# A decoder layer on one core: rounding attention's output on VectorE, with the order around it changed

## Chip, core and metric

The kernel runs on one core of a Trainium2 chip. The metric is device time in microseconds (us) for one execution. Its engines are TensorE (PE in the profile; PEld are its weight loads), VectorE (DVE), ScalarE (ACT), GpSimd (POOL) and SyncE (SP), which issues all transfers here. Each engine takes its instructions in program order and waits on semaphores for the others.

## What is computed

One pre-norm decoder layer on x of 8 batches x 112 tokens x 512, with a context of 8 x 375 x 512. Only the second sublayer matters here: two attentions of 16 heads of 128 (8 groups of two heads) over quantised projections, "own" over the 112 tokens and "context" over the 375, whose outputs are divided by a smoothing vector, rounded to 8-bit floats and projected together.

```python
def _div_clamp_fp8(x, scale):
    y = jnp.clip(x.astype(jnp.float32) / scale, -448.0, 448.0)
    y = y.astype(jnp.bfloat16).astype(jnp.float32)
    return y.astype(jnp.float8_e4m3fn).astype(jnp.float32)
...
core = _gqa(q, k, v).reshape(b, s, nh * d)       # own
xout = _gqa(qx, kx, vx).reshape(b, s, nh * d)    # context
cat = jnp.concatenate([core, xout], axis=-1)
catq = _div_clamp_fp8(cat, proj_smooth)
return jnp.einsum('bsi,oi->bso', catq, wproj) * (proj_in_scale * proj_w_scale)
...
x = x + _L0_attn_ref(_layernorm(x), ...)
x = x + _L0_xattn_ref(_layernorm(x), ctx_2048, ...)
x = x + _L0_ffn_ref(_layernorm(x), ...)          # silu(gate) * up, rms norm, down; ternary weights
```

## The kernel before

The program runs in stages. First attention and the quantising of its normed output (to about 180 us), then 32 *own* units (to about 460 us), 32 *context* units (to about 1,080 us), a short drain of the last ones, and the feed-forward part with its final scaling and stores.

**Units.** Unit i is head pair-of-groups s = i // 8 and batch b = i % 8. Eight units of one s are called a block here. The 896 tokens make 7 tiles of 128 (NT = 7), so a tile overlaps two batches: projection, normalising and rounding go by tiles (b = 7 has none, and the first unit of a block has no finished tile to round), scores and softmax by batches. While unit g projects, older units are advanced: `advance(stage, g)` runs that stage for each live unit that is far enough (the number beside the stage's name in `stages`). The calls stand in `Own.project` and `Context.project`; since the order is written out by hand, their order is the order of every engine's instructions.

**One own unit g before, in order.** Project q (8 matmuls of 512 columns); *rounded* of unit g-4; *normed* of g-1 (ACT: six scalings, one copy of v); statistics of q (DVE, L173 and L174); *score* of g-2 (4 matmuls, then the maximum, L847); *out* of g-5 (8 matmuls, then the addition to x, L713); *turn_p* of g-3 (transposes of the probabilities, ACT copy L866); project k and v; statistics of k, then powers on POOL (L184, L187, L133, L189); *weigh* of g-2 (four exponentials on ACT, L855, reciprocal L736 on DVE, product L738 on POOL); *attend* of g-3 (2 matmuls, `smoothed` on DVE, L747); *turn* of g-1 (transposes of q and k, L725 and L828; ACT makes qT, L730; DVE makes kT, L833); then `own_background`, which splits weight chunks of 128 x 512 into a high and a low part, and `form_parts`, which prepares the context in DRAM (ACT L1058, POOL L1059, DVE L1065). A chunk (s, what, k) has what = 0 (q), 1 (k and v) or 2 (output). Chunks with what = 2 cost ACT L300 and POOL L301; the others ACT L309 and DVE L310; those of what = 1 of the context (s > 3) ACT L293, POOL L294 and, a unit later in `split_end`, DVE L284 and ACT L285.

**Rounding before** (`rounded`, with `round_begin` and `round_a`): ACT takes the absolute value of y, scaled, into `big` (L203); DVE clips y (L207) and clips `big` (L208); POOL adds (L210) and subtracts (L758), which gives `cq`, the left operand of *out*'s matmuls.

**Buffers and queues.** PSUM has four banks with the tag ps and four with the tag pa. A ps tile takes the bank whose last use was released first, so the transposes of k (L828) wait for L713 of the same unit. Weight chunks are loaded by SP in the order of `queue`, one per finished split, five ahead.

**Drain and feed-forward.** After the last unit three passes run the remaining stages; `between` puts `ffn_input(0)` (norm, transposes, split of the feed-forward's input for the first four tiles) and four `hidden_part` calls among them, and `ffn_input(1)` follows. In the last `down`, the root-mean-square factor `rstd` comes from POOL, and DVE then does two instructions per tile (L1414 scales the partial sum and adds x, L1415 adds the last product), seven tiles, each stored at once.

Of the kernel before, what the change touches and what calls it, by code (L numbers as in the profile page):

```python
# [39 lines left out]
def decoder_layer(  # L40
# [210 lines left out]
    for s in range(8):  # L251
        if s == 4:

            for b in range(B - 1):
                queue += made.get(b, [])
                queue += [(4, 2, b)] if b < 2 else [(4, 2, 2), (4, 2, 3)] if b == 2 else [(5, 1, b - 3)]
            queue += [(5, 0, k) for k in range(KC)]
            continue
        queue += [(s, 2, k) for k in range(KC)]
        if s == 3:  # L260
            queue += [(4, 0, 0), (4, 1, 0), (4, 0, 1), (4, 0, 2), (4, 0, 3), (4, 1, 1), (4, 1, 2), (4, 1, 3)]
        elif s < 3:
            queue += [(s + 1, 1, 0), (s + 1, 1, 1), (s + 1, 0, 0), (s + 1, 0, 1)]
            queue += [(s + 1, 0, 2), (s + 1, 0, 3), (s + 1, 1, 2), (s + 1, 1, 3)]
        elif s < 7:
            queue += [(s + 1, what, k) for what in (1, 0) for k in range(KC)]

# [105 lines left out]
    with ExitStack() as st:  # L373
# [199 lines left out]
            nc.vector.tensor_mul(lnb[:, cut], rins[:, cut], vec[:, V_LNB : V_LNB + 4])  # L573
        rsm = const.tile([P, 32], F32, tag="rsm", name="rsm")
        nc.vector.reciprocal(rsm, vec[:, V_SM : V_SM + 32])
        nc.vector.tensor_scalar_mul(rsm[:, 0:16], rsm[:, 0:16], vec[:, V_SC + 2 : V_SC + 3])
        psc = const.tile([P, 1], F32, tag="psc", name="psc")
        nc.vector.tensor_mul(psc, vec[:, V_SC + 5 : V_SC + 6], vec[:, V_SC + 4 : V_SC + 5])
# [161 lines left out]
    def smoothed(u, po):  # L740

        po3 = po[:, :SH].rearrange("p (h s) -> p h s", s=S)
        r = rsm[:, 4 * u.s : 4 * u.s + 4].rearrange("p (h o) -> p h o", o=1)
        for t, rows, cut in batch_pieces(u.b):
            if (u.s, t) not in ys_:
                ys_[u.s, t] = w2.tile([P, 4, P], BF, tag="f8y", name=uid("y"), bufs=3)
            nc.vector.tensor_tensor(  # L747
                ys_[u.s, t][:, :, rows], po3[:, :, cut],
                r.to_broadcast([P, 4, cut.stop - cut.start]), ALU.mult,
            )  # L750

    def rounded(u):
        if u.b == 0:
            return
        y = ys_.pop((u.s, u.b - 1)).rearrange("p h s -> p (h s)")
        t, big = round_a(*round_begin(y, w2, 2), w2, 2)
        u.cq = w2.tile([P, 4 * P], F32R, tag="cq", name=uid("cq"))
        nc.gpsimd.tensor_tensor(u.cq, t, big, ALU.subtract)  # L758

    class Unit:  # L760

# [5 lines left out]
    class Own(Unit):  # L767
# [5 lines left out]
        def project(self, g):  # L773
            tile_ = self.b < NT
            tokens = slice(self.b * P, (self.b + 1) * P)
            if tile_:
                project_q(self, lambda k: xq[0][:, k, tokens])
                if self.i == 0:
                    quantise_turn(KC)
            advance("rounded", g)  # L780
            advance("normed", g)
            if tile_:
                heads = self.heads = Heads("own", P, 6)
                heads.stats(*[self.pq[:, j * P : (j + 1) * P] for j in range(4)])
            advance("score", g)
            advance("out", g)
            advance("turn_p", g)
            self.pkv = pa()
            for m in (0, 1) if tile_ else (1,):
                rows, n = (tokens, P) if m == 0 else (slice(self.b * S, (self.b + 1) * S), S)  # L790
                cut = slice(m * 256, (m + 1) * 256)
                for k in range(KC):
                    both(
                        self.pkv[:n, cut], xq[1 + m][:, k, rows], split[self.s, 1, k], cut,
                        k == 0, k == KC - 1,
                    )
            if self.b == NT:
                drop(self.s, 1)
            if tile_:
                heads.stats(*[self.pkv[:, j * P : (j + 1) * P] for j in range(2)])  # L800
                heads.powers([(4, epsc[:, 0:1]), (2, epsc[:, 1:2])])
            advance("weigh", g)
            advance("attend", g)
            advance("turn", g)
            if self.i < 4 * B - 1:
                own_background(self.s, self.b)
            form_parts(self.i)
# [275 lines left out]
    def own_background(s, b):  # L1083

        split_end()
        if s > 0 and b < 4:
            split_chunk(s, 2, b)
        elif s == 0 and b == 3:
            split_chunk(s, 2, 0)
            split_chunk(s, 2, 1)  # L1090
        elif s == 0 and b in (4, 5):
            split_chunk(s, 2, b - 2)
        if s < 3 and b in (4, 5):
            split_chunk(s + 1, 1, b - 4)
        if s == 3:
            for what, k in {4: ((0, 0), (1, 0)), 5: ((0, 1), (0, 2)), 6: ((0, 3), (1, 1)), 7: ((1, 2), (1, 3))}.get(b, ()):
                split_chunk(4, what, k)
                if b == B - 1:
                    split_end()
            return  # L1100
        if b >= 5:
            split_chunk(s + 1, 0, b - 5)
        if b == 7:
            split_chunk(s + 1, 0, 3)
            split_chunk(s + 1, 1, 2)
            split_chunk(s + 1, 1, 3)


    NU = FF // 256
# [103 lines left out]
                nc.gpsimd.tensor_scalar_mul(d[k], ts[k // 2][:, k % 2, :], 2.0)  # L1213
        wfs[what, i] = d

    def ffn_input(half):
        cols = CUTS[half]
        n, hs = cols.stop - cols.start, []
        for i in range(n // P):
            t = cols.start // P + i  # L1220
            h = f0.tile([P, H], F32, tag="sg", name=uid("h"), bufs=4)
            norm_apply(h, xs[t], *stats3[t])
            hs.append(h)
        for k in range(KC):
            tp = ps()
            for i, h in enumerate(hs):
                nc.tensor.transpose(tp[:, i * P : (i + 1) * P], h[:, k * P : (k + 1) * P], ident)
            hi, lo = [ring.tile("AB", "h3T", n) for _ in range(2)]
            nc.scalar.copy(hi, tp[:, :n])
            nc.vector.tensor_tensor(lo, tp[:, :n], hi.bitcast(F32), ALU.subtract)  # L1230
            hT[half, k] = hi, lo
# [124 lines left out]
    def hidden(u, pool):  # L1356
# [3 lines left out]

    hidden(0, f0)

    between = {
        (1, "score"): lambda: ffn_input(0),
        (2, "out"): lambda: hidden_part(0, 0, 0),
        (2, "turn_p"): lambda: hidden_part(0, 1, 0),
        (2, "rounded"): lambda: hidden_part(1, 0, 0),
        (3, "out"): lambda: hidden_part(1, 1, 0),
    }
    for n in range(1, 4):  # L1370
        live = [v for v in live if v.at < len(v.stages)]
        for stage in ("normed", "weigh", "out", "turn_p", "attend", "turn", "rounded", "score"):
            advance(stage, len(units) - 1 + n)
            if (n, stage) in between:
                between[n, stage]()

    attention.close()
    f1 = ctx.enter_context(tc.tile_pool(name="f1", bufs=1))
    tpool.append(ctx.enter_context(tc.tile_pool(name="tern2", bufs=1)))
    ffn_input(1)  # L1380
    expand_w("down", 0)
    ys = [f1.tile([P, H], F32, tag=f"y{t}", name=f"y{t}") for t in range(NT)]
    def down(c, hid, last):
        wd, pos = wfs.pop(("down", c)), []
        for t in range(NT):
            po = ps()
            for k in range(4):
                for part_ in range(2):
                    nc.tensor.matmul(  # L1389
                        po,  # L1390
                        lhsT=hid[part_][:, k, t * P : (t + 1) * P],
                        rhs=wd[k],
                        start=(k == 0 and part_ == 0),
                        stop=(k == 3 and part_ == 1),
                    )
            if c == 0:
                nc.vector.tensor_copy(ys[t], po)
            elif not last:
                nc.vector.tensor_tensor(ys[t], ys[t], po, ALU.add)
            else:  # L1400
                pos.append(po)
            if last and t == 1:
                pr = ps()
                for i in range(NT):
                    nc.tensor.matmul(
                        pr[:, i : i + 1], lhsT=sq[:, i * P : (i + 1) * P], rhs=ones1, start=True, stop=True
                    )
                rstd = sm("rms", NT)
                nc.vector.tensor_scalar(rstd, pr[:, 0:NT], 1.0 / FF, RMS_EPS, ALU.mult, ALU.add)
                power(rstd)  # L1410
            while last and t > 0 and pos:
                i = t + 1 - len(pos)
                r = rstd[:, i : i + 1]
                nc.vector.scalar_tensor_tensor(ys[i], ys[i], r, xs[i], ALU.mult, ALU.add)  # L1414
                nc.vector.scalar_tensor_tensor(ys[i], pos.pop(0), r, ys[i], ALU.mult, ALU.add)  # L1415
                nc.sync.dma_start(out=out[i * P : (i + 1) * P, :], in_=ys[i])

# [120 lines left out]
```

## Time and profile before

| what | before |
|---|---|
| median of 3 runs | 1285.07 us (1284.45 to 1289.41) |
| profiled execution | 1283.86 us, span 1282.1 us |
| granted TensorE clock, mean | 0.975 |
| L828 in own unit 9 to L828 in own unit 17 | 267.11 to 334.55 us |
| L828 in own unit 17 to that in own unit 25 | 334.55 to 401.89 us |
| L207 (clip of y), 128x512, between 215 and 460 us | x25, mean 1076 ns, 26.9 us |
| L210 and L758 (POOL's two steps of rounding), 128x512 | x56 each, mean 1240 and 1164 ns |

A group line of the profile reads: line, engine, operation, output tile <- input tiles, shapes, count | busy us, mean ns | idle time of the engine just before these instructions and what ended it. A row of the timeline reads: start in us, duration in us, engine, line, operation, tiles and shapes, count [idle before it <- what ended the idle]. A duration includes what an instruction waits after it has begun. A row of the waits reads: who waited <- for whom: us in total, times, longest.

### The profile page before, as it was taken

To read this page: it belongs to the slowest core of one execution; us is meant where nothing else is said; L and a number is where in the kernel's file an instruction comes from. 1 tells how busy PE (TensorE), PEld (TensorE's weight loads), DVE (VectorE), ACT (ScalarE), POOL (GpSimd) and SP (SyncE) were. 2 spreads that over 40 slices of the span, in tenths; PEclk is the share of its full clock that TensorE was granted. 3 is DMA by queue.
4 is the path that set the end of the run, shared out by engine and by line. 5 is a ranking of instruction groups with operands and counts; after the bars stand their busy time and mean duration, and the time that the engine had idled before them with its cause. 6 is when DMAs were issued, how large, how long until landed. Compare 5 with 4: busy or idle time off the path is not lost. (4 is left out here: it accounts for less than half of the span.)

```text
span 1282.1 us, 19634 instructions
## 1 busy us (share of the span) xinstructions
PE 1200.6 (94%) x6326; PEld 962.4 (75%) x6326; DVE 931.8 (73%) x2366; ACT 815.8 (64%) x2008; POOL 846.1 (66%) x938
## 2 busy tenths in 40 slices
PE   8997976889999889999999999999999998899998
PEld 5673765777888767888788778788777786687876
DVE  6647986887888866677776776677777775579864
ACT  2334676878687757667667767777667665456432
POOL 6657866687877756765767656667566655477762
PEclk9988886999999999999999999999999999999999
DMA  5001120213332354455554455554544440133201
GB/s 172 1 1 42 34 91 17 83 50 106 131 127 93 122 209 152 147 201 194 182 174 151 151 171 174 162 170 161 174 150 148 167 157 5 34 107 104 73 29 58
DMA packets 55511, 149.85 MB, mean 117 GB/s; under 512 B 6400, under 2 KB 15744, under 8 KB 55408
## 3 DMA queue, kind: packets, MB, share of 16 engines
q1 hardware_dynamic: 55408, 148.59, 35.3%
q8 instruction: 50, 0.82, 0.3%
q14 instruction: 53, 0.43, 0.1%
HBM read 120.18 MB, written 26.56 MB: 114 GB/s over the span
## 5 line engine op out<-in xcount | busy, mean ns | idle before, releaser
L912 PE MATMUL pa<-wx,ct 128*125 128x512 f32 x1152 | 289.4, 400 | 2.4 <-ACT wx L293 1.5
L912 PEld LDWEIGHTS pa<-wx,ct 128*125 128x125 f32 x1152 | 208.9, 186 | 51.2 <-ACT wx L293 1.9
L210 POOL TENSOR_TENSOR f8t<-y,big 128x512 f32<-128x512 bf16 (+1 forms) x88 | 107.4, 1224 | 140.2 <-DVE big L208 139.8
L738 POOL TENSOR_TENSOR p<-p,ri 112x448 f32<-112x448 f32 (+1 forms) x64 | 118.1, 1846 | 35.6 <-DVE ri L736 35.4
L923 DVE TENSOR_TENSOR kv<-kv,pa 125x512 f32<-125x512 f32 x96 | 65.9, 687 | 98.7 <-PE pa L912 52.2
L691 PE MATMUL pa<-hi,xq 128*128 128x512 f32 (+2 forms) x352 | 112.9, 345 | 11.0 <-DVE xq L368 9.2
L997 ACT ACTIVATE p<-ps,cmx 112x375 f32<-112x375 f32 x128 | 71.8, 574 | 75.5 <-DVE cmx L996 75.5
L1256 PE MATMUL pa<-h3T,wf 128*128 128x512 f32 (+1 forms) x512 | 110.0, 371 | 2.7 <-DVE sg L1266 2.7
L691 PE MATMUL pa<-lo,xq 128*128 128x512 f32 (+2 forms) x352 | 107.5, 331 | 0.9 <-DVE lo L310 0.9
L1256 PEld LDWEIGHTS pa<-h3T,wf 128*128 128x128 f32 x512 | 92.9, 188 | 14.9 <-DVE sg L1266 3.6
L174 DVE BATCH_NORM_AGGREGATE mv<-bst 128x2 f32<-128x6 f32 (+1 forms) x472 | 86.0, 182 | 16.3
L691 PE MATMUL ps<-hi,cq 128*128 128x512 f32 x224 | 90.8, 405 | 2.8 <-POOL cq L758 1.1
L730 ACT ACTIVATE qT<-ps,hln 128x448 f32<-128x448 f32 (+6 forms) x112 | 57.4, 567 | 56.1 <-PE ps L725 55.8
L691 PE MATMUL ps<-lo,cq 128*128 128x512 f32 x224 | 88.4, 395 | 0.0
L173 DVE BATCH_NORM_STATS2 bst<-pa 128x6 f32<-128x128 f32 x280 | 76.2, 272 | 16.2 <-PE pa L691 16.2
L988 PE MATMUL ps<-kT,qT 128*112 128x375 f32 x256 | 86.0, 478 | 0.5 <-ACT kT L974 0.5
L1158 POOL TENSOR_TENSOR th<-th,tw 128x512 bf16<-128x512 bf16 x48 | 59.1, 1231 | 40.1 <-DVE th L1150 40.1
L193 ACT ACTIVATE kv<-kv,ckvnm,ckvr 125x128 f32<-125x128 f32 x192 | 77.5, 491 | 6.2 <-POOL ckvnm L189 5.5
L691 PEld LDWEIGHTS pa<-hi,xq 128*128 128x128 f32 (+1 forms) x352 | 67.9, 193 | 17.3 <-DVE xq L368 10.7
L1021 PE MATMUL ps<-pT,kv 125*128 125x224 f32 x384 | 78.0, 353 | 0.0
L1021 PEld LDWEIGHTS ps<-pT,kv 125*128 125x128 f32 x384 | 72.6, 190 | 2.0
L691 PEld LDWEIGHTS pa<-lo,xq 128*128 128x128 f32 (+1 forms) x352 | 68.0, 193 | 7.4 <-DVE lo L310 3.8
(181 smaller groups left out, 3131.1 us busy)
## 6 DMA issues: line engine op xcount, KB each, us to landing
ct<-forms SPq DMA_DIRECT2D x84, 750.0 KB, 4.4
w<-in_wattn SPq DMA_DIRECT2D x96, 256.0 KB, 3.1
forms<-form SPq DMA_DIRECT2D x12, 750.0 KB, 4.7
forms<-ct SPq DMA_DIRECT2D x12, 750.0 KB, 5.1
tr<-in_wgu SPq DMA_DIRECT2D x32, 256.0 KB, 4.5
done<-th SPq DMA_DIRECT2D x48, 128.0 KB, 4.3
wh<-done SPq DMA_DIRECT2D x24, 256.0 KB, 3.7
tr<-in_wdown SPq DMA_DIRECT2D x16, 256.0 KB, 4.4
```

The source lines that it names most:

```text
L173: nc.vector.bn_stats(st[: self.rows], a)
L174: nc.vector.bn_aggr(self.mv[: self.rows, self.at, :], st[: self.rows])
L193: nc.scalar.activation(dst, src, AF.Identity, bias=self.nm[:rows, i : i + 1], scale=self.r[:rows, i : i + 1])
L210: nc.gpsimd.tensor_tensor(t, y16, big, ALU.add)
L691: nc.tensor.matmul(out_, lhsT=lhsT, rhs=part[:, cut], start=first and i == 0, stop=last and i == 1)
L738: nc.gpsimd.tensor_tensor(u.p, u.p, bc, ALU.mult)
L912: nc.tensor.matmul(banks[bank][:CJ, :], lhsT=ct[:, at : at + CJ] if ct.dtype == F32R else ct[:, at : at + CJ].bitcast(F32R), rhs=split[sel ...
L923: nc.vector.tensor_tensor(kv, kv, banks[1][:CJ, :], ALU.add)
L988: nc.tensor.matmul(pp[:S, :SC], lhsT=qT[:, j, :], rhs=self.kT[:, j // 2, :], start=True, stop=True,)
L997: nc.scalar.activation(self.p[:, j, :], pp[:S, :SC], AF.Exp, bias=nm[:S], accum_out=self.sums[:S, j : j + 1])
L1021: nc.tensor.matmul(po[:, cut], lhsT=self.kv[j][:, 256 + g * P : 256 + (g + 1) * P], rhs=self.pT[:, j, cut], start=(j == 0), stop=(j == NJ ...
L1256: nc.tensor.matmul(pp[:, :n], lhsT=wcur[k][:, m * 256 + blk * P : m * 256 + (blk + 1) * P], rhs=hT[half, k][i], start=(k == 0 and i == 0), ...
```

## The change

The rounding's clip and absolute value move to the end of `smoothed` (stage *attend*), for every unit whose tile is complete. `rounded` then has two DVE instructions with two operations each: `t = max(big, c) + y` and `cq = max(big, c) - t`. POOL does nothing in it. That difference is the negative of the rounded value, so the reciprocal smoothing vector is negated once at the start. The upper clip of `big` is dropped, as y is clipped before the absolute value is taken.

In an own unit *out* now comes ahead of *score*, and *turn* ahead of *attend*. The weight splits get a table, `split_plan`: each unit of blocks 1 and 2 has at most two chunks (before, the last of a block had four), and block 3 splits the context's k and v chunks before its q chunks; `queue` is put in the same order. In the drain, `ffn_input` is cut into `input_norms`, `input_turns` (transposes tile by tile into four held banks) and `input_splits`, and these are put between the stages. In the last `down`, tiles 3 to 6 are scaled on ACT and added to x on POOL, so that DVE has one instruction left for each.

```diff
-        queue += [(s, 2, k) for k in range(KC)]
...
+        if s < 3:
+            queue += [(s, 2, 0), (s, 2, 1), (s, 2, 2), (s + 1, 1, 0), (s, 2, 3), (s + 1, 1, 1)]
+            queue += [(s + 1, 0, k) for k in range(KC)] + [(s + 1, 1, 2), (s + 1, 1, 3)]
+            continue
...
+        nc.vector.tensor_scalar_mul(rsm, rsm, -1.0)
...
 def smoothed(u, po):
...
+        if u.b > 0:
+            y = ys_[u.s, u.b - 1]
+            nc.vector.tensor_scalar(y, y, 448.0, -448.0, ALU.min, ALU.max)
+            y = y.rearrange("p h s -> p (h s)")
+            ys_[u.s, u.b - 1] = round_begin(y, w2, 2)
 def rounded(u):
...
-        y = ys_.pop((u.s, u.b - 1)).rearrange("p h s -> p (h s)")
-        t, big = round_a(*round_begin(y, w2, 2), w2, 2)
+        y, big = ys_.pop((u.s, u.b - 1))
+        t = w2.tile([P, 4 * P], F32, tag="f8t", name=uid("f8t"))
+        nc.vector.scalar_tensor_tensor(t, big, 1.5 * 2.0**14, y, ALU.max, ALU.add)
         u.cq = w2.tile([P, 4 * P], F32R, tag="cq", name=uid("cq"))
-        nc.gpsimd.tensor_tensor(u.cq, t, big, ALU.subtract)
+        nc.vector.scalar_tensor_tensor(u.cq, big, 1.5 * 2.0**14, t, ALU.max, ALU.subtract)
...
 class Own, project
+            advance("out", g)
             advance("score", g)
-            advance("out", g)
...
             advance("weigh", g)
+            advance("turn", g)
             advance("attend", g)
-            advance("turn", g)
...
+    for s in range(4):
+        plan = {b: [(s, 2, b)] for b in range(4)} if s else {3: [(0, 2, 0), (0, 2, 1)], 4: [(0, 2, 2)], 5: [(0, 2, 3)]}
+        n = s + 1
+        if s < 3:
+            plan[2 if s else 4] += [(n, 1, 0)]
+            plan[3 if s else 5] += [(n, 1, 1)]
+            if s:
+                plan |= {4: [(n, 0, 0)], 5: [(n, 0, 1)], 6: [(n, 0, 2), (n, 0, 3)], 7: [(n, 1, 2), (n, 1, 3)]}
+            else:
+                plan |= {6: [(n, 0, 0), (n, 0, 1)], 7: [(n, 0, 2), (n, 0, 3), (n, 1, 2), (n, 1, 3)]}
+        else:
+            plan |= {4: [(4, 1, 0), (4, 1, 1)], 5: [(4, 1, 2), (4, 0, 0)], 6: [(4, 1, 3), (4, 0, 1)], 7: [(4, 0, 2), (4, 0, 3)]}
...
+    input_norms(0, 1)
+    last(1, "normed", "weigh")
+    input_norms(2, 3)
+    last(1, "out")
+    input_turns(0, 0, 1, 2, 3)
+    last(1, "turn_p", "attend", "turn", "rounded")
+    input_splits(0)
+    last(1, "score")
+    hidden_part(0, 0, 0)
+    last(2, "weigh")
+    hidden_part(0, 1, 0)
+    last(2, "turn_p", "out", "attend")
+    input_norms(4, 5)
+    last(2, "rounded")
+    hidden_part(1, 0, 0)
+    input_turns(1, 4, 5)
+    last(3, "out")
+    input_norms(6)
+    hidden_part(1, 1, 0)
...
+    input_turns(1, 6)
+    input_splits(1)
...
+                for i in range(3, NT):
+                    nc.scalar.activation(ys[i], ys[i], AF.Copy, scale=rstd[:, i : i + 1])
+                    nc.gpsimd.tensor_tensor(ys[i], ys[i], xs[i], ALU.add)
...
-                nc.vector.scalar_tensor_tensor(ys[i], ys[i], r, xs[i], ALU.mult, ALU.add)
+                if i < 3:
+                    nc.vector.scalar_tensor_tensor(ys[i], ys[i], r, xs[i], ALU.mult, ALU.add)
                 nc.vector.scalar_tensor_tensor(ys[i], pos.pop(0), r, ys[i], ALU.mult, ALU.add)
```

More of the change, by code (lines that the diff above doesn't have):

```diff
@@ L258, in decoder_layer @@
             continue
+        if s < 3:
+            queue += [(s, 2, 0), (s, 2, 1), (s, 2, 2), (s + 1, 1, 0), (s, 2, 3), (s + 1, 1, 1)]
+            queue += [(s + 1, 0, k) for k in range(KC)] + [(s + 1, 1, 2), (s + 1, 1, 3)]
+            continue
         queue += [(s, 2, k) for k in range(KC)]
         if s == 3:
[L261 to L264, printed above, removed]
+            queue += [(4, 1, 0), (4, 1, 1), (4, 1, 2), (4, 0, 0), (4, 1, 3), (4, 0, 1), (4, 0, 2), (4, 0, 3)]
         elif s < 7:
@@ L1085, in own_background @@
         split_end()
[L1086 to L1106, printed above, removed]
+        for n, what, k in split_plan[s].get(b, ()):
+            split_chunk(n, what, k)
+    split_plan = []
+    for s in range(4):
[10 more added lines that the diff above has]
+            plan |= {4: [(4, 1, 0), (4, 1, 1)], 5: [(4, 1, 2), (4, 0, 0)], 6: [(4, 1, 3), (4, 0, 1)], 7: [(4, 0, 2), (4, 0, 3)]}
+        split_plan.append(plan)
     NU = FF // 256
@@ L1214, in expand_w, with input_norms, input_turns, input_splits @@
         wfs[what, i] = d
[L1216 to L1220, printed above, removed]
+    inputs = {}
+    def input_norms(*ts):
+        for t in ts:
             h = f0.tile([P, H], F32, tag="sg", name=uid("h"), bufs=4)
             norm_apply(h, xs[t], *stats3[t])
[L1223 to L1227, printed above, removed]
+            inputs[t] = h
+    def input_turns(half, *ts):
+        first = CUTS[half].start // P
+        if ts[0] == first:
+            inputs["banks", half] = [f() for f in ((ps, ps, pa, pa) if half else (pa,) * KC)]
+        for t in ts:
+            h = inputs.pop(t)
+            for k, tp in enumerate(inputs["banks", half]):
+                nc.tensor.transpose(
+                    tp[:, (t - first) * P : (t - first + 1) * P], h[:, k * P : (k + 1) * P], ident
+                )
+    def input_splits(half):
+        n = CUTS[half].stop - CUTS[half].start
+        for k, tp in enumerate(inputs.pop(("banks", half))):
             hi, lo = [ring.tile("AB", "h3T", n) for _ in range(2)]
@@ L1361, in decoder_layer, with last @@
     hidden(0, f0)
[L1363 to L1372, printed above, removed]
-            advance(stage, len(units) - 1 + n)
-            if (n, stage) in between:
-                between[n, stage]()
+    def last(n, *stages):
+        for stage in stages:
+            advance(stage, len(units) - 1 + n)
+    live = [v for v in live if v.at < len(v.stages)]
+    input_norms(0, 1)
[17 more added lines that the diff above has]
+    hidden_part(1, 1, 0)
+    assert not any(v.at < len(v.stages) for v in live)
     attention.close()
@@ L1379, in decoder_layer @@
     tpool.append(ctx.enter_context(tc.tile_pool(name="tern2", bufs=1)))
-    ffn_input(1)
+    input_turns(1, 6)
+    input_splits(1)
     expand_w("down", 0)
```

## The prediction

> **What bounds the kernel now.** I read the page's shares first, then the busy time by 20 us windows, then the waits of 215 to 460 us, then the timeline of single own units.
>
> ```profile
> PE 1200.6 (94%) x6326; PEld 962.4 (75%) x6326; DVE 931.8 (73%) x2366; ACT 815.8 (64%) x2008; POOL 846.1 (66%) x938
> ...
> L207 DVE TENSOR_SCALAR y<-y 128x512 bf16<-128x512 bf16 x25 | 26.9, 1076 | 8.1 <-ACT big L203 8.1
> ...
> 500.00:520.00 20.00, 20.00 (x99) 16.28 (x98) 13.64 (x40) 14.96 (x38) 14.87 (x16) 1.00 0.50 171
> ```
>
> TensorE is the bound of the context stage: the window from 500 us shows it busy for all 20 us, and its idle time from 500 to 1060 us sums to 5 us. The 81 us that it idles lie elsewhere: some 22 us in the own units from 215 to 460 us, 8 us in the drain (1078 to 1122 us), the rest at the start and the end. The own units are what the change rewrites. There the second line is odd: a clip that takes 0.28 us when undisturbed has a mean of 1.08 us. The timeline of own unit 18, with POOL's rows behind DVE's, says why:
>
> ```profile
> 344.10 0.18 DVE L736 RECIPROCAL ri<-sum 112x4 f32<-112x4 f32 x1
> 346.56 3.15 DVE L207 TENSOR_SCALAR y<-y 128x512 bf16<-128x512 bf16 x1 [0.55 <-ACT big L203]
> 349.63 0.28 DVE L208 TENSOR_SCALAR big<-big 128x512 bf16<-128x512 bf16 x1
> 351.45 0.59 DVE L847 TENSOR_REDUCE mx<-ps 112x4 f32<-112x448 f32 x1
> 351.96 0.74 DVE L713 SCALAR_TENSOR_TENSOR x<-ps,psc,x 128x512 f32<-128x512 f32 x1
> 353.62 0.18 DVE L736 RECIPROCAL ri<-sum 112x4 f32<-112x4 f32 x1
> ...
> 346.16 0.94 POOL L738 TENSOR_TENSOR p<-p,ri 112x448 f32<-112x448 f32 x1
> 347.06 1.28 POOL L301 TENSOR_TENSOR lo<-w,hi 128x512 fp32r<-128x512 f32 x1
> 348.30 1.26 POOL L1059 TENSOR_TENSOR form<-raw,form 128x500 fp32r<-128x500 f32 x1
> ```
>
> The clip begins at 346.56 and ends when POOL's third instruction ends (349.56): DVE is held while POOL works, through instructions that follow each other. So the unit is a loop through three engines: maximum (L847), four exponentials, reciprocal (L736), POOL's product, split and form, the clips, four statistics, the next maximum. From one reciprocal to the next it takes 9.52 us; TensorE's own work in such a unit is 8.3 us (start to start of its groups, without waits).
>
> I check this reading by summing units 17 to 24 by hand, each as its loop from maximum to maximum: 1.58 us to the reciprocal, 1.25 for L747 and L833, then splits and the wait for ACT and POOL, 0.4 for two clips, 1.62 for the statistics, 0.59. With nothing in the way that is 5.6; held by L738 and one split 8.25, by a form too 9.65. The eight are 8.25, 9.65, 9.65, 5.6 (no rounding), 8.45, 8.6, 6.9 and 9.5: 66.6 us. Measured between L828 at 334.55 and at 401.89: 67.3. So the loop, not TensorE's 60.9 us, sets an own block.
>
> **The change, own units.** POOL loses L210 and L758, 1.24 and 1.16 us in 56 tiles, 134 us of its work. None of it is in the loop, because both come after the clips and *out* is a unit later. DVE loses L208 and gains two two-operation instructions per tile. No row has them; L1414 (f32, 0.74) and L1150's least (16-bit, 0.69) bound them, so 0.72 each, 0.78 from start to start where the second needs the first (L1414 to L1415). That is 1.2 us more per tile.
>
> What matters is where they stand. The clip, then ACT's absolute value, then both new instructions, then the statistics are now one chain: from the maximum, 2.83 us to the clip, 0.2 clip, 0.65 absolute value (L203), 1.5 for the pair, 1.62 statistics, 0.66 for L713 (now ahead of the maximum), 0.59, and some 0.05 per handover: 8.1 us where it was 5.6. That is TensorE's 8.3 with nothing to spare. Two things lengthen it further. The splits' high parts (L300, L309) now stand behind the absolute value on ACT, and L310 stands on DVE ahead of the pair: a q chunk puts the pair back by 1.35 us, a chunk in two halves by 1.3, and a form's L1065 by 0.65. And the pair has two SBUF inputs each, which POOL holds up as well:
>
> ```profile
> 301.81 0.48 DVE L310 SCALAR_TENSOR_TENSOR lo<-w,vec,hi 128x256 fp32r<-128x256 f32 x1
> 302.21 1.16 DVE L310 SCALAR_TENSOR_TENSOR lo<-w,vec,hi 128x256 fp32r<-128x256 f32 x1
> ...
> 301.90 1.19 POOL L738 TENSOR_TENSOR p<-p,ri 112x448 f32<-112x448 f32 x1
> ...
> 460.99 2.38 DVE L284 SCALAR_TENSOR_TENSOR wx<-wx,w 128x512 fp32r<-128x512 f32 x1
> ...
> 460.64 0.93 POOL L738 TENSOR_TENSOR p<-p,ri 112x448 f32<-112x448 f32 x1 [1.78 <-DVE ri L736]
> 461.53 1.28 POOL L294 TENSOR_TENSOR w<-w,wx 128x512 f32<-128x512 f32 x1
> ```
>
> Two like instructions follow each other at 301.81 and 302.21, POOL asks at 301.90, and the second waits behind it (1.16 for 0.48 us of work). The L284 waits through two POOL instructions. After the change POOL's split asks 0.6 us after the absolute value ends, while the first of the pair still runs, so the second of the pair waits 1.28 us, 2.5 with a form.
>
> Units 17 to 24 without any hold: 8.3, 8.3, 10.55, 7.0, 8.8, 10.1, 8.55, 10.95, in all 72.6, that is +5 against 67.3. With every hold: 10.3, 10.8, 12.8, 7.0, 10.1, 10.15, 9.75, 10.9, in all 81.8, +14. The rows with f32 inputs speak for the second; a 16-bit instruction with two inputs (L1148 at 1140.50, 1.27 us) got in between two of POOL's. I take 9 per block: 27 for the last three, and 3 for the three roundings of units 5 to 7. Ends: 15 and 48; the end below nothing is the first rival.
>
> The Trainium skill ("SBUF — State Buffer", section "Who interferes with whom") says that a VectorE instruction with two SBUF inputs contends with a GpSimd instruction that reads SBUF, and that the second to issue blocks until the first finishes. The rows go further: the wait lasted through two or three POOL instructions. By the rule's single wait the units with a form would lose 1.28 instead of 2.5, and my 30 would be some 23.
>
> What is gained: *out* ahead of *score* and kT ahead of `smoothed` take away "PE ps L841 <- DVE kT L833", 7.4 us in six waits. In a loop bound by DVE, TensorE then waits at the transposes of k for L713 instead. I count nothing.
>
> **Seam to context.** Now the q chunks 2 and 3 come last: *project q* of unit 32 waits for `smoothed`, clip, absolute value, two L309 and two L310, to 464.3 by the same rows, then twelve L912 without the two waits of 1.48 and 0.90 before: 467.2 against 467.4. Nothing.
>
> **Context.** 1.2 us more on DVE in 28 units, covered by DVE's idle time ahead of L923 (98.7 us, 3.1 per unit). ACT's qT and kT (L730, L974) now stand behind the absolute value and so behind the clip; where POOL's L1158 and L1159 (2.4 us) hold the clip, *score* is late by some 0.4. Ends 0 and 8; I take +1, since keys(2) lies between with 3 us of TensorE's work. SP has the same transfers in the order of use.
>
> **Drain.** Before, TensorE's waits are 2.54, 0.49, 1.14, 0.18, 1.12, 1.64 and 0.36: 7.5 us. The first is for POOL's product (2.69 us):
>
> ```profile
> 1082.77 1.56 PE L1009 MATMUL ps<-ident,p 112*125 112x112 f32 x12 [2.54 <-POOL p L738]
> ```
>
> Sixteen transposes (2.96 us) now fill it, but two norms may be held behind that product: 0.7 left of 2.54. 1.14, 0.18 and 1.12 go. *score* waits for a kT that is now behind the absolute value: 1.5 for 0.49. The last transposes end at once in four banks, the next part needs the third bank's split, 2.1 for 2.0. Sum 4.3, so -3 (ends -5 and 0).
>
> **End.** Four of DVE's L1414 (0.75) go to ACT and POOL. If POOL's four additions (1.3 each by L1245) alternate with the two L1414 left, the end is 2.1 us earlier; if they hold the second L1414 through, as L284 was held, tiles 1 and 2 are late, TensorE waits for their banks, and the end is 1.1 later. By that nearest row, +1.
>
> **Sum.** 30 + 0 + 1 - 3 + 1 = +29 on the profiled execution's 1283.86 (span 1282.1 and 1.8 around it) is 1313; the median of the runs lies 1.2 above that execution: 1314.
>
> **Rivals.** (1) *Own units run at TensorE's pace.* If POOL, freed of 134 us, is done before DVE asks, and ACT takes the absolute value without delay, the loop of 8.1 hides under 8.3. At most 19 us are there (three blocks of 67.3 to 60.9); half of it, with 3 of the drain and 2 of the end, gives 1285 - 15 = 1270. For it: POOL is 75% busy there and waits end on it. Against: DVE's own work per block, start to start, rises from 48 to 57 us, and each split adds a handover. It decides if L207's place shows under 0.5 us. Chance 0.20. (2) *A wash*: half of the low end's 15 and the gains cancel, 1279 to 1291. Chance 0.10. (3) *Every hold, and the context's ACT too*: 48 + 8 + 1, 1342. Chance 0.08. Forecast, 1296 to 1338: 0.62.
>
> **Range and chances.** About 0.5% (6 us) is what a measurement here tells from no change. Faster 0.20, same 0.10, slower 0.70. From 1274, which leaves out half of the first rival, to 1338, which leaves out the third. The forecast's own range is 1296 to 1338.
>
> **What would show it.** In the profile after: L828 to L828 of a block 72 to 82 us (wrong below 67); the second of the pair with a mean over 1.2 us in own units and durations of 2 to 3 us beside L301 and L1059; DVE over 85% busy from 215 to 460 us; TensorE's waits there on L713 rather than kT; the drain's wait on L738 below 1 us; 11.7 us from the end of POOL's power for `rstd` to DVE's last instruction (10.6 before). The forecast falls if the pair runs at 0.7 us each and the statistics start on TensorE's word.

## The result, and the profile after

The changed kernel takes 1352.59 us (median of 4 runs, 1350.85 to 1355.58) against 1284.76 beside it: ratio 1.0527, 95% interval 1.0505 to 1.055. It is slower, as forecast, but by 68 us where 29 were predicted, and outside the range. The profiled execution took 1352.46 us (span 1350.7).

Stage by stage in the two profiles, each from the start of one landmark on TensorE to the start of the next, the last to the end of the span (us):

| stage | before | after | difference | predicted |
|---|---|---|---|---|
| own: transposes of k in unit 1 to the first key matmul | 280.5 | 328.4 | +47.9 | +30 |
| seam: to the first context score | 32.8 | 33.3 | +0.5 | 0 |
| context: to the start of the last group of key matmuls | 577.6 | 603.0 | +25.4 | +1 |
| drain: to the first feed-forward matmul | 24.8 | 20.0 | -4.8 | -3 |
| the rest | 185.2 | 184.7 | -0.5 | +1 |

The page after, section 1 and the clock line of section 2, and then the clock line of before:

```profile
PE 1232.5 (91%) x6326; PEld 982.7 (73%) x6326; DVE 994.8 (74%) x2419; ACT 819.2 (61%) x2012; POOL 720.0 (53%) x830
...
PEclk9997778889988978999999999999999999999999
```
```profile
PEclk9988886999999999999999999999999999999999
```

VectorE has 63 us more, POOL 126 us less. TensorE does the same 6326 matmuls and is busy for 32 us more: slices 8 to 15 of the clock line, counted from 0 (270 to 540 us), all showed 9 before and now have 7 and 8 among them. That was in no step of the prediction; what it costs is taken up below.

The groups of VectorE from 215 to 500 us, in the columns of the group line:

```profile
L765 DVE SCALAR_TENSOR_TENSOR f8t<-big,y 128x512 f32<-128x512 bf16 x25 | 27.9, 1118 | 3.0 <-ACT big L203 2.8
L767 DVE SCALAR_TENSOR_TENSOR cq<-big,f8t 128x512 fp32r<-128x512 bf16 x25 | 25.8, 1032 | 0.9
L756 DVE TENSOR_SCALAR y<-y 128x512 bf16<-128x512 bf16 x25 | 7.2, 290 | 0.1
```

The clip is rid of its hold (1076 to 290 ns), and the pair has it instead: in context units the same two instructions take 692 ns each. The timeline of an own unit shows how:

```profile
358.60 0.28 DVE L756 TENSOR_SCALAR y<-y 128x512 bf16<-128x512 bf16 x1
...
358.92 0.63 ACT L203 ACTIVATE big<-y 128x512 bf16<-128x512 bf16 x1 [0.74 <-DVE y L756]
359.59 0.69 DVE L765 SCALAR_TENSOR_TENSOR f8t<-big,y 128x512 f32<-128x512 bf16 x1 [0.70 <-ACT big L203]
360.14 1.28 POOL L302 TENSOR_TENSOR lo<-w,hi 128x512 fp32r<-128x512 f32 x1 [0.46 <-ACT hi L301]
360.31 1.66 DVE L767 SCALAR_TENSOR_TENSOR cq<-big,f8t 128x512 fp32r<-128x512 bf16 x1
361.38 1.71 POOL L1068 TENSOR_TENSOR form<-raw,form 128x500 fp32r<-128x500 f32 x1
```

POOL's L302 begins while the first of the pair runs, and the second waits for it: 1.66 us for 0.69 of work. But it slips in between L302 and L1068, and then L1068 waits (1.71 instead of 1.26 us). Here the form does not add to the hold: 1.66, where the prediction had 0.72 plus 2.5. The units at 430 and 440 us show the same. Elsewhere the pair waits through two of POOL's instructions that follow each other (the rows below, and 2.64 us for the first of the pair at 349.55) or three (3.96 at 465.06), and five times a form alone holds one of the pair, for 1.63 to 1.76 us:

```profile
269.94 2.70 DVE L767 SCALAR_TENSOR_TENSOR cq<-big,f8t 128x512 fp32r<-128x512 bf16 x1
...
269.93 0.93 POOL L741 TENSOR_TENSOR p<-p,ri 112x448 f32<-112x448 f32 x1
270.82 1.26 POOL L302 TENSOR_TENSOR lo<-w,hi 128x512 fp32r<-128x512 f32 x1
```

The windows of one own block (columns as in the prediction's window; the number after POOL's is the granted clock), before and after:

```profile
334.50:401.90 67.40, 62.85 (x405) 54.49 (x404) 55.82 (x167) 52.81 (x164) 50.91 (x65) 1.00 0.34 116
```
```profile
353.20:434.70 81.50, 70.18 (x404) 61.14 (x403) 63.89 (x180) 53.29 (x164) 37.20 (x53) 0.90 0.27 94
```

The block lasts 14.1 us longer. In TensorE's account, its idle time grows from 4.6 to 11.3, that is 6.8 us, and the same matmuls take 7.3 us more at a clock of 0.90. In VectorE's account, 8.1 us more are busy and 6.0 more idle; it is busy for 78% of the block, not for over 85%.

Which account tells what sets the pace is seen from whom VectorE waits for. The windows of all of own, before and after, then VectorE's waits in them:

```profile
181.18:461.70 280.52, 244.54 (x1535) 210.97 (x1534) 227.82 (x661) 216.21 (x652) 211.36 (x261) 0.96 0.28 95
...
DVE bst L173 <- PE pa L691: 13.9, 12, 2.3
...
DVE lo L310 <- ACT hi L309: 4.5, 9, 0.7
```
```profile
181.29:509.69 328.40, 267.81 (x1534) 227.89 (x1533) 255.90 (x689) 219.12 (x655) 158.88 (x212) 0.89 0.24 82
...
DVE ri L739 <- ACT p L864: 25.9, 28, 2.0
DVE lo L311 <- ACT hi L310: 23.4, 19, 1.6
DVE bst L173 <- PE pa L694: 8.6, 7, 2.4
```

Of own's 47.9 us VectorE is busy for 28.1 (its holds included) and idle for 19.8. Its waits for ScalarE grow from 24.6 to 52.1 us: for the exponentials ahead of L739, and for the high parts of weight splits, which now stand behind the absolute value. Its waits for TensorE shrink from 16.8 to 10.2. So own is paced by VectorE with ScalarE and POOL, and nothing here shows that TensorE's lower clock lengthens it.

In the context TensorE was never idle for long before (19.1 to 20.0 us busy in each 20 us window from 500 to 1060 us); now such windows from 540 to 1140 us show it busy for 17.4 to 20.0, and its idle time grows from 5.9 to 24.1 us. The waits from 543 to 1146 us (total, times, longest):

```profile
ACT big L203 <- DVE y L756: 87.9, 25, 6.2
...
PE ps L997 <- ACT kT L983: 19.1, 18, 2.6
```

And a unit of it in the timeline:

```profile
657.01 2.07 DVE L311 SCALAR_TENSOR_TENSOR lo<-w,vec,hi 128x512 fp32r<-128x512 f32 x3
659.00 0.68 DVE L750 TENSOR_TENSOR y<-ps,rsm 128x320 bf16<-128x320 f32 x2
659.59 0.28 DVE L756 TENSOR_SCALAR y<-y 128x512 bf16<-128x512 bf16 x1
...
659.91 0.63 ACT L203 ACTIVATE big<-y 128x512 bf16<-128x512 bf16 x1 [6.15 <-DVE y L756]
660.45 1.00 ACT L733 ACTIVATE qT<-ps,hln 128x64 f32<-128x64 f32 x2
...
661.35 0.66 ACT L983 ACTIVATE kT<-ps,hln 128x375 f32<-128x375 f32 x1
...
662.06 2.24 PE L997 MATMUL ps<-kT,qT 128*112 128x375 f32 x4 [2.56 <-ACT kT L983]
```

ScalarE stands still for 6.15 us ahead of the absolute value, because VectorE still works on ternary steps (L1148 to L1155) and weight splits (L311) queued ahead of `smoothed`. qT and kT, whose transposes ended long before, come behind it, and *score* waits 2.56 us.

### The profile page after: what moved, and what is told of

Same layout as the page of the kernel before. It is cut to its first block, busy times and chain, and to the rows that moved or that the text cites. A ratio compares the mean times of both kernels' runs of the same rounds, so it can differ in the third digit from the quotient of the medians.

```text
span 1350.7 us, 19583 instructions
## 1 busy us (share of the span) xinstructions
PE 1232.5 (91%) x6326; PEld 982.7 (73%) x6326; DVE 994.8 (74%) x2419; ACT 819.2 (61%) x2012; POOL 720.0 (53%) x830
## 5 line engine op out<-in xcount | busy, mean ns | idle before, releaser
L921 PE MATMUL pa<-wx,ct 128*125 128x512 f32 x1152 | 291.9, 402 | 0.0
L741 POOL TENSOR_TENSOR p<-p,ri 112x448 f32<-112x448 f32 (+1 forms) x64 | 116.9, 1827 | 75.4 <-DVE ri L739 58.1
L203 ACT ACTIVATE big<-y 128x512 bf16<-128x512 bf16 (+1 forms) x88 | 53.9, 612 | 129.2 <-DVE y L756 127.5
L694 PE MATMUL pa<-hi,xq 128*128 128x512 f32 (+2 forms) x352 | 119.2, 362 | 11.2 <-DVE xq L369 9.2
L184 POOL TENSOR_SCALAR ckvr<-mv 125x6 f32<-125x6 f32 x32 | 9.3, 290 | 198.4 <-DVE mv L174 198.4
L694 PE MATMUL pa<-lo,xq 128*128 128x512 f32 (+2 forms) x352 | 112.1, 342 | 0.0
L997 PE MATMUL ps<-kT,qT 128*112 128x375 f32 x256 | 90.9, 499 | 20.6 <-ACT kT L983 20.6
L694 PE MATMUL ps<-lo,cq 128*128 128x512 f32 x224 | 92.4, 412 | 0.1
L997 PEld LDWEIGHTS ps<-kT,qT 128*112 128x112 f32 x256 | 44.7, 180 | 57.9 <-ACT kT L983 28.7
L694 PEld LDWEIGHTS pa<-hi,xq 128*128 128x128 f32 (+1 forms) x352 | 71.2, 202 | 17.4 <-DVE xq L369 10.7
L864 ACT ACTIVATE p<-ps,mx 112x112 f32<-112x112 f32 x128 | 43.9, 360 | 62.0 <-DVE mx L856 62.0
L184 POOL TENSOR_SCALAR ownr<-mv,epsc 128x4 f32<-128x4 f32 (+1 forms) x56 | 17.2, 307 | 120.4 <-DVE mv L174 112.3
```

The lines of the kernel that those rows point to most:

```text
L203: nc.scalar.activation(big, y16, AF.Abs, scale=2.0**20)
L694: nc.tensor.matmul(out_, lhsT=lhsT, rhs=part[:, cut], start=first and i == 0, stop=last and i == 1)
L741: nc.gpsimd.tensor_tensor(u.p, u.p, bc, ALU.mult)
L921: nc.tensor.matmul(banks[bank][:CJ, :], lhsT=ct[:, at : at + CJ] if ct.dtype == F32R else ct[:, at : at + CJ].bitcast(F32R), rhs=split[sel ...
L997: nc.tensor.matmul(pp[:S, :SC], lhsT=qT[:, j, :], rhs=self.kT[:, j // 2, :], start=True, stop=True,)
```

## The experiments

Twelve kernels. "Own" and "context" are the stages of the table above, from each kernel's profile; before has 280.5 and 577.6, after 328.4 and 603.0.

| kernel | us | ratio to before, 95% interval | own | context |
|---|---|---|---|---|
| ctx_begin_late | 1347.4 | 1.0494 (1.0444 to 1.0545) | 328.3 | 598.1 |
| begin_late | 1355.4 | 1.0548 (1.0512 to 1.0584) | 334.7 | 597.5 |
| pool_rounding | 1291.1 | 1.0044 (1.0019 to 1.0068) | 291.9 | 577.2 |
| seams_alone | 1280.7 | 0.996 (0.9938 to 0.9982) | 281.3 | 577.5 |
| dead_pair | 1412.7 | 1.0974 (1.0955 to 1.0994) | 352.6 | 633.3 |
| pool_quiet | 1328.0 | 1.0311 (1.0287 to 1.0334) | 306.8 | 598.8 |
| order_back | 1351.0 | 1.0497 (1.0469 to 1.0526) | 328.8 | 602.5 |
| order_alone | 1285.1 | 0.9985 (0.9963 to 1.0007) | 285.1 | 577.5 |
| ctx_pair_last | 1337.3 | 1.0417 (1.0393 to 1.0441) | 326.8 | 582.8 |
| own_pair_late | 1322.1 | 1.0297 (1.0272 to 1.0321) | 297.4 | 600.9 |
| splits_alone | 1281.5 | 0.9967 (0.9951 to 0.9982) | 285.5 | 577.2 |
| pairs_late | 1308.8 | 1.0159 (1.0117 to 1.0201) | 297.3 | 582.8 |

**Which part of the change costs: pool_rounding and seams_alone.** The first keeps everything but the rounding:

```diff
-        nc.vector.tensor_scalar_mul(rsm, rsm, -1.0)
...
+        y = ys_.pop((u.s, u.b - 1)).rearrange("p h s -> p (h s)")
+        t, big = round_a(*round_begin(y, w2, 2), w2, 2)
...
+        nc.gpsimd.tensor_tensor(u.cq, t, big, ALU.subtract)
```

> The changed kernel with the old rounding (both clips on VectorE and POOL's sum and difference, all in *rounded*; the sign is not turned); stage order, split table, queue, drain and end stay as changed. Theory (the rounding alone costs what own and context lost): own and context stages within 5 us of before, drain and end keep 4 and 2: 1278 us (1272 to 1284). Rival (the order of stages or the split table costs by itself, or holds TensorE at its own pace): over 1290, or below 1270.

The second is the kernel before with the new drain (`input_norms`, `input_turns`, `input_splits`, `last`) and the new end alone.

> The kernel before with only the drain's new order (norms, transposes, splits of the feed-forward's input between the stages) and the end's four tiles on ACT and POOL. Theory (they give what the landmarks of the changed kernel show, 4.9 and 2.1 us less, 0.8 back at the second half): 1278 to 1280, ratio 0.995. Rival (they gained only because the changed kernel came to the drain in another state): 1284 to 1286.

The rounding costs 61 of the 68 us: with the old rounding, context is back at 577.2 and own at 291.9. seams_alone is faster than both kernels (interval below 1): 5.8 us less in the drain, 1.9 us less from the start of the last matmul to the end (6.2 to 4.3), and 3.1 us lost again between the first feed-forward matmul and the first of `down`. pool_rounding's own expectation (1278, own within 5 us of before) missed: it stays 10 us above seams_alone, its rival's "over 1290", with own 11.4 longer than before. So order and table were taken one by one.

**Order and split table: order_back, order_alone, splits_alone.**

```diff
             advance("score", g)
             advance("out", g)
...
             advance("attend", g)
             advance("turn", g)
```

> The changed kernel with own units' stages in the order of before (score ahead of out, attend ahead of turn). Theory (out's addition ahead of the maximum lengthens the loop that sets an own unit; pool_rounding lost 10 us with it): 1338 to 1347. Rival (as the prediction had it, the order is worth nothing in a loop set by VectorE): 1350 to 1355. Second rival (attend ahead of turn puts qT behind the absolute value on ScalarE as well): over 1358.

> seams_alone (the kernel before with the new drain and end, 1280.7 us) with own units' new order of stages alone. Theory (the order is what pool_rounding lost): 1288 to 1293. Rival (the split table and its queue are what it lost): 1279 to 1283. In between, both.

> seams_alone (1280.7 us) with the new split table and queue alone. Theory (pool_rounding is 10 us above seams_alone, of which the order of stages is 3 to 4, so the table costs the rest): 1285 to 1289. Rival (order and table cost only together): 1279 to 1283.

Undone in the changed kernel, the order is worth nothing (own 328.8): the prediction's reading, here the first rival. The window of its own stage, to set beside the two above:

```profile
178.63:507.45 328.82, 258.02 (x1535) 219.34 (x1533) 264.90 (x689) 218.75 (x655) 158.20 (x212) 0.93 0.25 82
```

Own is as long as in the changed kernel, while the clock is 0.93 instead of 0.89 and TensorE is busy for 9.8 us less: what the clock gives back turns into idle time. On VectorE two things trade places: its wait for the exponentials falls from 25.9 to 12.0 us, and the second of the pair takes 1597 instead of 1032 ns, in three units beside a form 3.94 us. Alone on seams_alone it comes to 1285.1, between the two expectations, and the intervals overlap; its own stage is 3.8 us longer. The table alone costs nothing in all, as its rival had it: 4.2 us more in own, most of it in the last block (63.4 against 60.4), where the context's q chunks now come last, and 2.7 less in the seam. What the two cost together beyond that was not followed further.

**Whether POOL's hold on the pair costs: pool_quiet.**

```diff
-            nc.gpsimd.tensor_tensor(lo, w, hi.bitcast(F32), ALU.subtract)
+            nc.gpsimd.memset(lo.bitcast(F32), 0.0)
...
-        nc.gpsimd.tensor_tensor(f[:, 2, :], w, f[:, 0, :].bitcast(F32), ALU.subtract)
+        nc.gpsimd.memset(f[:, 2, :].bitcast(F32), 0.0)
```

> The changed kernel, with POOL's differences for the output projection's weight chunks and for the context's forms (L302 and L1068) replaced by a fill with zeros that reads nothing, so that the low parts of these weights and the middle part of the forms are left out. Theory (those differences hold the pair: its means of 1.12 and 1.03 us in own units against 0.69 in context units): the means fall under 0.8, own units give back 10 to 20 us, 1332 to 1343. Rival (the hold only stands where VectorE would have waited anyway): 1348 to 1353.

Own falls by 21.6 us, the whole by 24.6, more than expected. The pair's groups from 215 to 500 us:

```profile
L765 DVE SCALAR_TENSOR_TENSOR f8t<-big,y 128x512 f32<-128x512 bf16 x25 | 23.2, 927 | 3.0 <-ACT big L203 2.8
L767 DVE SCALAR_TENSOR_TENSOR cq<-big,f8t 128x512 fp32r<-128x512 bf16 x25 | 18.0, 720 | 0.9
```

The second is all but free (0.69 us in 24 of 25 units); the first still meets POOL's product L741 and, once, the context weights' L295 (3.96 us), so its mean stays over the 0.8 expected. Both together give up 12.5 us of waiting, and L311, which has two tensor inputs as well, 8.7. VectorE's busy time in own falls by 20.2 us and its waits for ScalarE stay as they were, so the hold by these differences is worth some 20 of own's 47.9. The fill also takes POOL 0.52 us where the difference took 1.28, which this run doesn't separate, but TensorE's wait for POOL's product stays as it was (8.1 us after, 7.6 here). The Trainium skill ("SBUF — State Buffer", section "Who interferes with whom") says that a GpSimd instruction that only writes SBUF doesn't contend with a two-input VectorE instruction; the fills agree.

**Whether the chain or VectorE's time costs: dead_pair.** pool_rounding, and VectorE runs the pair as well, for nobody:

```diff
+        t = w2.tile([P, 4 * P], F32, tag="f8t", name=uid("dead"))
+        nc.vector.scalar_tensor_tensor(t, big, 1.5 * 2.0**14, y, ALU.max, ALU.add)
+        nc.vector.scalar_tensor_tensor(t, big, 1.5 * 2.0**14, t, ALU.max, ALU.subtract)
```

> pool_rounding (old rounding with the new order and splits, 1291.1 us), and in *rounded*, behind POOL's sum, VectorE runs the two two-operation instructions as well, into a tile that nobody reads. Theory (VectorE's occupancy is the cost: whatever stands behind the pair in its queue, maxima and reciprocals, comes later): two instructions of some 0.7 us or more per tile bring back at least half of the 61 us between pool_rounding and the changed kernel, 1322 to 1350. Rival (the chain from clip through ScalarE's absolute value to the pair and on to the projection is the cost; work that nobody waits for goes into VectorE's idle time): 1290 to 1305.

122 us on top of pool_rounding, twice the most that the first theory allowed. The timeline of a context unit says why it overshoots:

```profile
712.73 0.69 DVE L762 SCALAR_TENSOR_TENSOR dead<-big,y 128x512 f32<-128x512 bf16 x1
712.78 1.65 POOL L210 TENSOR_TENSOR f8t<-y,big 128x512 f32<-128x512 bf16 x1 [3.21 <-DVE big L208]
713.46 1.53 DVE L763 SCALAR_TENSOR_TENSOR dead<-big,dead 128x512 f32<-128x512 bf16 x1
```

The dead pair collides with POOL's own rounding, which the pair of the change doesn't. So its size can't be read across. What it does show: work whose result nobody waits for lengthens own by 61 us and context by 56. VectorE's idle time did not absorb it; how much of that is VectorE's queue and how much POOL's rounding held up, this run doesn't separate.

**The context: ctx_begin_late, begin_late, ctx_pair_last.** In the first, for context units:

```diff
-        if u.b > 0:
+        if u.b > 0 and u.s < 4:
+            begin(u)
...
     def rounded(u):
+        if not (u.s < 4):
+            begin(u)
```

`begin` is the clip and the absolute value. begin_late does so for all units.

> The changed kernel, but in context units the clip and the absolute value stand at the start of *rounded* again, behind *turn*; own units stay as changed. Theory (in context units ACT's qT and kT queue behind an absolute value that waits for VectorE's queue): the context stage gives back its 26 us, 1327 us (1322 to 1332), ACT's wait L203 <- y falls from 97 to under 20 us in all and the wait of score for kT from 19 to under 3. Rival (VectorE's 1.2 us more per unit and the pair itself cost the 26 us): 1345 to 1353, and the wait for kT moves to another name.

> The changed kernel, with clip and absolute value at the start of *rounded* in all units, so that VectorE itself stands still between clip and pair while ACT takes the absolute value. Theory (in own units the chain clip, absolute value, pair, statistics is what costs, wherever it begins): as ctx_begin_late within 8 us, 1319 to 1335, with the clip's mean back above 0.8 us. Rival (what costs is that the weight splits stand between the absolute value and the pair): 1300 to 1312.

The theory fell: 5 us, not 26. The wait it spoke of did go, and another took its place. TensorE's waits of ctx_begin_late from 548 to 1146 us:

```profile
PE ps L1023 <- POOL p L741: 14.7, 15, 2.6
...
PE ps L1002 <- ACT kT L988: 1.7, 1, 1.7
```

The timeline of one unit of it, followed down to that wait:

```profile
643.80 0.69 DVE L770 SCALAR_TENSOR_TENSOR f8t<-big,y 128x512 f32<-128x512 bf16 x1 [0.70 <-ACT big L203]
...
644.53 0.69 DVE L772 SCALAR_TENSOR_TENSOR cq<-big,f8t 128x512 fp32r<-128x512 bf16 x1
645.14 0.68 DVE L285 SCALAR_TENSOR_TENSOR wx<-wx,w 128x512 fp32r<-128x512 f32 x1
645.74 0.68 DVE L937 TENSOR_TENSOR kv<-kv,pa 125x512 f32<-125x512 f32 x1
...
647.28 1.88 DVE L1010 TENSOR_REDUCE cmx<-ps 112x1 f32<-112x375 f32 x4
...
650.25 0.18 DVE L739 RECIPROCAL ri<-sum 112x4 f32<-112x4 f32 x1 [1.10 <-ACT p L1011]
...
650.58 2.69 POOL L741 TENSOR_TENSOR p<-p,ri 112x1500 f32<-112x1500 f32 x1 [0.95 <-DVE ri L739]
...
653.32 2.49 PE L1023 MATMUL ps<-ident,p 112*125 112x112 f32 x12 [1.66 <-POOL p L741]
```

From the pair to the maxima VectorE has no gap. Its idle time (98.7 us before, ahead of the addition to kv) lies behind the maxima; the pair stands ahead of them. So maxima, exponentials, reciprocal, POOL's product and the next unit's transposes all come later by the pair. begin_late stands 8.05 us above ctx_begin_late, at the edge of the 8 that its theory allowed; its clip takes 444 ns in own units, not over 0.8 us, and own is 6.3 us longer than in the changed kernel. Its rival (1300 to 1312) is out. The test of the new reading:

```diff
             advance("turn", g)
-            advance("rounded", g)
+            for u in live:
+                if u.s > 3 and u.b > 0 and u.at < len(u.stages) and u.stages[u.at][0] == "rounded":
+                    begin(u)
...
             advance("score", g)
+            advance("rounded", g)
```

> The changed kernel (1352.6 us), but in context units clip and absolute value stand behind *turn* and the pair behind *score*, so that neither ScalarE's qT and kT nor VectorE's four maxima have anything of the rounding ahead of them. Theory (in context units the maxima, and with them POOL's product for the next unit's transposes, come late because the pair stands ahead of them in VectorE's queue; VectorE has idle time, but behind the maxima): the context stage gives back most of its 26 us, 1327 to 1336, with TensorE's waits for kT and for POOL's product both under 6 us in all. Rival (VectorE's work per unit is the cost, wherever it stands): 1345 to 1353, as with clip and absolute value late alone (1347.4).

Context 582.8: 20.2 of 25.4 us are back, with the same two instructions per tile. TensorE's matmuls wait for kT no more, and those for POOL's product wait 4.9 us in all (4.7 before):

```profile
PE ps L1027 <- POOL p L741: 4.9, 9, 0.8
```

The time, 1337.3, lies 1 us above the expected range.

**Own units: own_pair_late, and both: pairs_late.**

```diff
-            advance("rounded", g)
             advance("normed", g)
...
-            advance("out", g)
             advance("score", g)
+            advance("rounded", g)
             advance("turn_p", g)
...
+            advance("out", g)
             advance("weigh", g)
```

> The changed kernel, but in own units *score* comes first, the pair behind the maximum, and *out* behind the projection of k and v, so that neither the statistics of q nor the maximum wait for absolute value and pair; the context stays as changed. Theory (what sets an own unit is the chain clip, absolute value, pair, statistics, addition, maximum, as the prediction summed it; and the pair meets POOL's differences there): own units give back 20 to 40 of 48 us, 1313 to 1333. Rival (VectorE's occupancy with the pair, held by POOL wherever it stands): 1345 to 1356.

> The changed kernel with both moves: in own units the pair behind the maximum and *out* behind the projection of k and v, in context units clip and absolute value behind *turn* and the pair behind *score*. Theory (two separate places in VectorE's queue, whose costs add): 1352.6 less 30.5 less 15.3, 1307 (1302 to 1312), still above before by what POOL's hold and VectorE's longer work leave. Rival (one limit behind both, so that the second move finds less to take): 1316 to 1323.

Own gives back 31 of 47.9 us when statistics and maximum no longer stand behind the pair. The pair meets POOL less there as well (841 and 719 ns), and VectorE's wait for the exponentials falls from 25.9 to 4.5 us, so this run doesn't divide the 31 between chain and hold. The two moves add up: 1308.8 against 1307. What is left, 17 us in own and 5 in context, was not divided.

## Why the prediction was right in sign and wrong in size

**The loop of an own unit** was read rightly: own_pair_late breaks it, and own falls by 31 us. The check by hand agrees with the trace before in sum (66.6, and 66.8 from maximum to maximum), but not unit by unit: units 17, 18 and 21 took 5.5, 11.4 and 10.4 us, where it has 8.25, 9.65 and 8.45.

**The size in own** failed at "I take 9 per block: 27 for the last three, and 3 for the three roundings", a choice in the middle between no hold (15 in all) and every hold (48). The four stretches lost 8.8, 9.8, 14.2 and 15.2 us. pool_quiet shows the hold at some 20 us, more than the 15 that the choice put on top of no hold, and own without POOL's differences still 26.3 us longer than before, where the sum without any hold had 15. What else was short is known in part: the first stretch lost 8.8 for 3; unit 20, which has no rounding, takes 9.2 us from maximum to maximum instead of 7.0, mostly since L311 is held there as well (2.42 us for two halves at 380.36) and the sum counted holds on the pair alone; and with the old rounding, order and split table by themselves make own 11.4 us longer, for which the sum had nothing (in the changed kernel the order is worth nothing, so this does not simply add).

That units 17 to 24 came to 81.5, next to the hand sum of 81.8 with every hold, is partly luck: where a split and a form follow each other the second of the pair waited once, not twice, as the 16-bit row at 1140.50 had shown, and unit 20 and waits in other places made up for it. The sum also took no account of TensorE's clock, which falls in own. TensorE's idle time grows by 24.6 us and what its clock loses by 20.4, but that is TensorE's account, and no run shows it as a cause: order_back has 9 us less of the second and the same length. The Trainium skill's rule of one wait (same section as above: the second to issue blocks until the first finishes) agrees with the 1.66 us at 360.31; the 2.70 and 3.96 us go beyond it, as the prediction's f32 rows did.

**"The seam to context: nothing"** held for the seam itself (+0.5). The last stretch of own lost 15.2 us; in pool_rounding, with the old rounding, it lost 8.5 already (68.3 for 59.8), and the split table alone accounts for 3.0 of that (splits_alone, 63.4 for the 60.4 of seams_alone).

**The context term failed outright**: "1.2 us more ... covered by DVE's idle time ahead of L923", ends 0 and 8, measured 25.4. The idle time was real and in the wrong place: an engine that takes its work in order can only use idle time that lies between the added work and what its followers wait for. The step had seen qT and kT queue behind the absolute value, but put POOL's hold as the reason (0.4 us); it was VectorE's whole queue of splits and ternary steps ahead of `smoothed`. And curing that alone gave 5 us, since the pair ahead of the maxima was next in line.

**Drain and end** were right within their ends: -4.8 and +0.7 (`down` starts 0.7 later, counted from the first feed-forward matmul) for -3; the end 2.1 us earlier (6.2 to 4.1 after the start of the last matmul), the end of the range that had POOL's additions alternate with VectorE, not the +1 taken.

**The order** was worth nothing in the changed kernel, as argued. Of the signs named, block length and waits on L713's successor (L716, 17.5 us at *attend*, against 1.6 for kT) came true, the second of the pair stayed at 1.03 us, below 1.2, and VectorE below 85%; from POOL's power for `rstd` to VectorE's last instruction it takes 8.5 us, not 11.7, and the drain's first wait for POOL's product is gone, while a later one, at 1175.48 us, takes 1.72. The third rival, every hold and the context's ScalarE too (48 + 8 + 1), was nearest; it had the own term to 0.1 us, by errors that offset each other, and a third of the context's.

## What to carry to other kernels

Idle time of an engine covers added work only if it lies between that work and the next instruction that somebody waits for: look in the timeline for where the idle time stands, not for its sum. When work moves to an engine in order, place it behind that engine's instructions on the critical loop; the same two instructions, with clip and absolute value behind *turn* both times, left context units 20 us longer than before ahead of the maxima and 5 behind them. And when a wait is removed, ask which one is next before counting it as gained.

## What the runs showed of the hardware

**Short waits bring TensorE's clock down.** After waits like those below its granted clock falls to 0.50. The windows of the changed kernel from 374 us, 1 us each, and TensorE's timeline there:

```profile
374.00:375.00 1.00, 0.00 (x0) 0.00 (x0) 0.93 (x6) 0.00 (x0) 0.00 (x0) 1.00 0.84 274
...
376.00:377.00 1.00, 0.53 (x1) 0.50 (x2) 1.00 (x3) 0.00 (x0) 0.20 (x1) 0.50 0.00 0
...
380.00:381.00 1.00, 1.00 (x4) 0.81 (x3) 0.64 (x1) 1.00 (x4) 1.00 (x2) 0.50 0.00 0
...
383.00:384.00 1.00, 1.00 (x6) 0.76 (x6) 0.94 (x4) 0.09 (x1) 0.00 (x0) 1.00 0.67 217
```
```profile
373.34 0.44 PE L837 MATMUL ps<-ident,k 128*128 128x128 f32 x2 [0.81 <-ACT pT L875]
376.47 1.86 PE L881 MATMUL ps<-pT,v 112*128 112x224 f32 x4 [2.69 <-DVE x L716]
...
380.69 0.63 PE L694 MATMUL pa<-hi,xq 128*128 128x512 f32 x1
...
383.29 0.40 PE L694 MATMUL ps<-lo,cq 128*128 128x512 f32 x1
```

Two waits of 0.81 and 2.69 us, and for 6.8 us (376.0 to 382.8) the clock is 0.50: a 512-column matmul lasts 0.63 instead of 0.40 us. From 215 us to the first context score there are ten such stretches after, one before; each lasts 3.4, 6.8 or 10.2 us. Busy time times the missing share of the clock, summed over 1 us windows of own, is 7.3 us before and 27.7 after; idle time is 35.9 and 60.5. This says where TensorE's time went, not what set the length: order_back, with own as long (328.8 for 328.4), has 19.0 us of clock loss and 70.8 of idle time. pool_quiet and own_pair_late, which shorten the waits, lose 17.8 and 13.5 us to the clock. Whether a part of own's loss is the clock's was not tested by itself.

The Trainium skill ("TensorE: Matmul & The Clock Gate", section "HAM oscillation — how this bites in real kernels") gives gaps of over about 3.4 us as those to avoid. Here waits of 2.69 and 0.81 us close together were enough, and before at 310.7 us, after waits of 0.22 and 1.58 us (308.4 and 310.4), the clock fell too, while a gap of 2.6 us that ended at 350.5 after brought nothing: no single length of a gap fits these three.
